# A graph, attention and experts layer on one core: conditional blocks placed inside two products, and rows of the experts' activations at 512-byte pitches

## The chip, the core and the metric

The kernel runs on one core of a Trainium2 chip. The profile names the core's engines PE (TensorE: matrix products; its weight loads are a row of their own, PEld), DVE (VectorE), ACT (ScalarE), POOL (GpSimd) and SP (SyncE, which here issues DMAs). An engine's own sequencer, which loads registers, compares and branches, is written with a q behind the name (PEq, DVEq). The metric is the device time of one execution in microseconds (us), lower being better; the kernel before took 1030.24 us, the median of three runs (1027.24 to 1032.03).

## The reference, cut to what matters

The input is a matrix x of 625 nodes by 1024, and 20000 edges `src -> dst`. Two sub-layers are added to x.

```python
xn = _layernorm(x, axis=-1)
x = x + _L0_gnn_ref(xn, src, dst, ...) + _L0_mix_ref(xn[None], Wq, Wk, Wv, Wo, bo)[0]
x = x + _L0_ffn_ref(_layernorm(x, axis=-1)[None], router_w, w1, w2, shared_gate_up, shared_down, shared_gate_w)[0]
```

`_L0_gnn_ref` is two graph layers: each is `h @ W_self + mean @ W_neigh + b`, where `mean` is the average of the rows of h over the incoming edges of a node, and the first is followed by a relu. `_L0_mix_ref` is a linear attention of 16 heads: q, k and v products, softmaxes, a small 64 x 64 context for each head, and an output product with Wo. `_L0_ffn_ref` is a mixture of 8 experts, of which each token takes two, `silu(x @ w1[e]) @ w2[e]`, beside a shared pair of products whose last one is `shared_down`. All weight matrices are 1024 x 1024 in float32.

## The kernel before, in words

**Products.** Every float32 operand is split into a rounded part and a remainder (`split`, L96 to L97: a copy on ACT makes `whi`, a subtraction on DVE makes `wlo`), and a product is three matmuls: high by high, high by low, low by high. Weights come in tiles of 128 x 1024 through one list, the stream `st` (L100 to L148): SP issues a tile's DMA, ACT and DVE split it, PE uses it. Three split tiles may exist at once, and the raw tiles are fetched three (in the experts six) ahead. `ts_half` (L197 to L210) multiplies the 625 nodes, in five tiles of 128 rows, by one half (512 columns) of a weight matrix. It has four steps u, one weight tile each, and in each step 30 matmuls of 512 columns, which add into five PSUM banks. There are eight banks in all. A caller may pass `step`, which is called behind each u.

**Order of the work around the change.** Queries and values are multiplied; a count of the edges becomes the matrix `ath`; `psc` (L725) and DVE's scaling (L728) make the contexts `cbd`. Then stands the first conditional block (L731), then `psa` (L742), which applies the contexts to the queries and is split into `aoh`, `aol`, then the output product with Wo (`pso`, both halves), whose banks are added to x and the biases in `xr` (POOL L760, DVE L761) and stored to `accd` in HBM. Then comes the neighbours' product (`neighbours`, L766; banks `psg`), which is split into `g0h`, `g0l`; then the second block (L776); then the hidden layer (`psag`, L802). The neighbours' product of the second layer follows, and then the product with its W_self (`psx`, L830). Its banks are added to `x2`, which holds what was stored in `accd` (L834, L835). The third block (L836) stands behind it, in front of `last_mean` (`psm`, L857). Later come the router, the shared gate and up products, the eight experts, a fourth block (L1255), and the last product with `shared_down` (`psz`).

**What the blocks are for.** Edge counts are packed in a few bits. `look` (L550) finds whether a count was too large for that, and puts a number into `rare`; every engine loads it into a register (L730) and branches. With the data of the run `rare` is 0, so the first three blocks are skipped: the first would count again (`recount`) and turn the inverse degrees around once more (`inverse`), the second and the third would add what the packed counts leave out (`low_part`). The fourth block is a loop over experts whose tokens don't fit into their slots; its number is loaded at L1254, and it runs once more `expert_narrow` with weights of its own. It is skipped as well. The first three blocks are written with `preferred_fallthrough_block=False`, the fourth without it. Two tiles of `shared_down` are split ahead of the fourth block (`st.ready`, L1253).

**Experts.** The six fuller experts run through `expert_wide` (L1135), three of them with n = 224 rows and three with 160; the other two have 128 rows and run through `expert_narrow` (L1210). In `expert_wide` the activations `he` are held for each of eight k as n columns of the high part followed by the low part: 2n float32 in a row, 1792 bytes for 224 and 1280 bytes for 160. For 160 the low part is cut so that the remaining 32 rows' high and low parts lie side by side. The second product (`psy`, L1184 and L1206 to L1208) loads slices of `he` as PE's weights and streams the weight tiles of w2. `expert_narrow` holds its `he` in pieces of 128 columns, 512 bytes each.

**What orders the instructions.** A framework (Tile) places the instructions on the engines' queues, gives out slots of shared buffers, and sets all semaphores. A conditional block is one unit for it. Slots are given out by tag: the large tiles (`xnh`, `xnl`, `hself`, `aoh`, `aol`, `g0h`, `g0l`, `hth`, `htl`, `x2`, `he` and others) share six, `tmp` has five.

Of the kernel before, what the change touches and what calls it, by code (L numbers as in the profile page):

```python
# [71 lines left out]
def gps_layer(ctx: ExitStack, tc: tile.TileContext, x, src, dst,  # L72
# [91 lines left out]
    def add_ts(w):  # L164
        for ap in row_aps(w):
            st.add(ap)
# [2 lines left out]
    add_ws(ws0)  # L169
    add_ts(wq)  # L170
    add_ts(wv)
    add_ts(wo)
    add_ts(wn0)
    add_ts(wn1)
    add_ts(ws1)
    for o in range(KT):
# [20 lines left out]
    def ts_half(xh, xl, accs, first=True, last=True, step=None):  # L197
        for u in range(4):
            wh, wl = st.next()
            for t in range(NT):  # L200
                c, acc = cols(t), accs[t][rows(t), :]
                for k in range(2):
                    kt = 2 * u + k
                    f = first and kt == 0
                    s = last and kt == KT - 1
                    nc.tensor.matmul(acc, xh[:, kt, c], wh[:, k, :], start=f, stop=False)  # L206
                    nc.tensor.matmul(acc, xh[:, kt, c], wl[:, k, :], start=False, stop=False)  # L207
                    nc.tensor.matmul(acc, xl[:, kt, c], wh[:, k, :], start=False, stop=s)  # L208
            if step:
                step(u)  # L210

    def ws_tile(xh, xl, accs, parts, last=True, w=None, step=None):
        wh, wl = w or st.next()
# [411 lines left out]
    def inverse(t0, n):  # L625
        ps = bank("psd").rearrange("p (a b) -> p a b", b=128)
        for t in range(n):
            p = rows(t0 + t)
            nc.tensor.transpose(ps[:, t, p], degs[p, 2, t0 + t:t0 + t + 1].to_broadcast([p.stop, 128]), ident[p, p])
        c = slice(t0 * T, min((t0 + n) * T, N))  # L630
        nc.scalar.copy(dinv[:, c], ps.rearrange("p a b -> p (a b)")[:, :c.stop - c.start])
# [89 lines left out]
    for o in range(KT):  # L721
# [4 lines left out]
        for h in range(2):  # L726
            r = slice(h * 64, (h + 1) * 64)
            nc.vector.tensor_scalar(cbd[r, o, r], ps[r, r], krs[r, o:o + 1], None, op0=ALU.mult)  # L728

    rare_v = nc.values_load(rare[0:1, 0:1], min_val=0, max_val=2)  # L730
    with tc.If(rare_v > 0, preferred_fallthrough_block=False):  # L731
        recount()
        inverse(0, NT - 1)
        inverse(NT - 1, 1)


    aoh, aol = slot_t("aoh"), slot_t("aol")
# [13 lines left out]
    for half in range(2):  # L751
        hs = slice(half * 512, (half + 1) * 512)
        accs = [bank("pso") for _ in range(NT)]
        ts_half(aoh, aol, accs)
        for t in range(NT):
            xr = tmp.tile([128, 512], F32, name="xr", tag="tmp")
            p = rows(t)
            for r, q in pieces(t):
                nc.gpsimd.dma_start(xr[q], x[r, hs])
            nc.gpsimd.tensor_add(xr[p], xr[p], bsum[p, hs])  # L760
            nc.vector.tensor_add(xr[p], accs[t][p, :], xr[p])  # L761
            for r, q in pieces(t):
                nc.gpsimd.dma_start(accd[r, hs], xr[q])


    def neighbours(xh, xl, gh, gl):  # L766
        for half in range(2):
            hs = slice(half * 512, (half + 1) * 512)
            accs = [bank("psg") for _ in range(NT)]
            ts_half(xh, xl, accs)  # L770
            for t in range(NT):
                split(accs[t][rows(t), :], gh[rows(t), t, hs], gl[rows(t), t, hs])

    g0h, g0l = slot_n("g0h", F32R), slot_n("g0l", F32R)
    neighbours(xnh, xnl, g0h, g0l)
    with tc.If(rare_v > 0, preferred_fallthrough_block=False):  # L776
        for s in range(NT):
            al = low_part(s)
            for o in range(KT):
                for c0, n in PARTS:  # L780
                    ps = bank("pslo")
                    c = slice(c0, min(c0 + n, N))
                    nc.tensor.matmul(ps[:, :n], g0h[rows(s), s, o * 128:(o + 1) * 128], al[rows(s), c0:c0 + n],
                                     start=True, stop=True)
                    lt = tmp.tile([128, NP], F32, name="lt", tag="tmp")
                    nc.vector.tensor_mul(lt[:, c], ps[:, :min(n, N - c0)], dinv[:, c])
                    nc.vector.tensor_add(hself[:, o, c], hself[:, o, c], lt[:, c])

    hth, htl = slot_t("hth"), slot_t("htl")
    pad(hth, htl)  # L790
# [33 lines left out]
    g1h, g1l = slot_n("g1h", F32R), slot_n("g1l", F32R)  # L824
    neighbours(hth, htl, g1h, g1l)
    x2 = slot_n("x2")
    for half in range(2):
        hs = slice(half * 512, (half + 1) * 512)
        accs = [bank("psx") for _ in range(NT)]
        ts_half(hth, htl, accs)  # L830
        for t in range(NT):
            p = rows(t)
            for r, q in pieces(t):
                nc.gpsimd.dma_start(x2[q, t, hs], accd[r, hs])  # L834
            nc.vector.tensor_add(x2[p, t, hs], accs[t][p, :], x2[p, t, hs])  # L835
    with tc.If(rare_v > 0, preferred_fallthrough_block=False):  # L836
        for s in range(NT):
            al = low_part(s)
            for t in range(NT):
                for half in range(2):  # L840
                    hs = slice(half * 512, (half + 1) * 512)
                    ps = bank("pslo")
                    p = rows(t)
                    nc.tensor.matmul(ps[p, :], al[rows(s), cols(t)], g1h[rows(s), s, hs], start=True, stop=True)
                    nc.vector.scalar_tensor_tensor(x2[p, t, hs], ps[p, :], degs[p, 2, t:t + 1], x2[p, t, hs],
                                                   op0=ALU.mult, op1=ALU.add)
    xst = const.tile([128, NT, 2, 6], F32, name="xst")
    def turn(tiles):
        for t in tiles:
# [285 lines left out]
    def expert_wide(row, n, xs, between):  # L1135

        rest = n - 128
        beside = rest <= 64
        he = big.tile([128, KT, 2 * n], F32R, name="he", tag="big")
        main, more = n + (rest if beside else 0), n + (0 if beside else 128)  # L1140
        for q in range(KT // 2):
            ps = [bank("pse") for _ in range(2)]
            for g in range(2):
                wh, wl = st.next()
                for a in range(2):
                    for k in range(4):
# [12 lines left out]
            for a in range(2):  # L1159
                nc.scalar.copy(s[:, a, :], ps[a][:, n:2 * n])  # L1160
                nc.vector.tensor_add(s[:, a, :], ps[a][:, :n], s[:, a, :])
            nc.scalar.activation(s, s, AF.Silu)
            h2 = he[:, 2 * q:2 * q + 2]
            if beside:
                nc.scalar.copy(h2[:, :, :n], s)
                for a0, b0, m in ((0, main, 128), (128, more, rest)):
                    nc.vector.tensor_sub(h2[:, :, b0:b0 + m], s[:, :, a0:a0 + m], h2[:, :, a0:a0 + m].bitcast(F32))
            else:
                split(s, h2[:, :, :n], h2[:, :, n:])
        r = between() if between else None  # L1170
        for half in range(2):
            accs = [bank("psy") for _ in range(2)]
            for u in range(4):
                wh, wl = st.next()
                rows_product(accs[0], lambda kt, p: he[:, kt, p * main:p * main + 128], u, wh, wl)
                if beside:

                    for k in range(2):
                        kt = 2 * u + k
                        f, e = kt == 0, kt == KT - 1  # L1180
                        both = (accs[1][:2 * rest], he[:, kt, 128:128 + 2 * rest], wh[:, k, :])
                        low = (accs[1][:rest], he[:, kt, 128:n], wl[:, k, :])
                        for m in (low, both) if e else (both, low):
                            nc.tensor.matmul(*m, start=f and m is both, stop=e and m is both)  # L1184
                else:
                    rows_product(accs[1][:rest], lambda kt, p: he[:, kt, 128 + p * n:n + p * n], u, wh, wl)
            expert_out(row, accs[:1], half, nc.vector.tensor_copy)
            y = tmp.tile([128, 512], F32, name="y", tag="tmp")
            if beside:
# [62 lines left out]
    st.load(st.used + st.ahead)  # L1252
    st.ready = [st.next(), st.next()]  # L1253
    n_over = nc.values_load(oi[0:1, OVB:OVB + 1], min_val=0, max_val=OVB)  # L1254
    with tc.If(n_over > 0):  # L1255
        with tc.For_i(0, n_over, 1) as j:
            ej = nc.values_load(oi[0:1, ds(j, 1)], min_val=0, max_val=NE - 1)
            row = REG + j * 128
# [58 lines left out]
```

## Time and profile before

| what | value |
|---|---|
| median of three runs | 1030.24 us (1027.24 to 1032.03) |
| the profiled execution | 1032.83 us, of which 1031.2 us are its span; 1.6 us lie around it |
| mean granted TensorE clock | 0.989 |
| PE, PEld, DVE, ACT, POOL busy | 1004.8, 866.2, 595.3, 397.7, 160.2 us |
| instructions | 14763 |
| `psc`, `psa`, `pso` | from 269.15, 279.08, 287.35 us of the span |
| first neighbours' product, hidden layer | from about 342, from 398.02 us |
| `psx` both halves, `last_mean` | from about 477, from 531.44 us |
| experts, last product | from about 680, from 970.12 us |

The span is the time from the first instruction to the last. A row of the groups gives a line of the kernel, the engine, the operation, the tiles written and read, its busy time, the mean duration of one, and the idle time ahead of it with what ended that. The view of waits says which engine waited for which other and for how long; "issue" there is idle time in which the profile shows nothing that the engine waited for. In the timeline the first column is the start and the second the length; matmuls overlap, so the time that one costs in a row of them is the distance between two starts. In the table by stretches each engine's busy time is followed by the granted TensorE clock (1.00 is full speed), the busy share of the DMA engines and the GB/s that they moved.

### The profile page before, as it was taken

To read this page: it belongs to the slowest core of one execution; us is meant where nothing else is said; L and a number is where in the kernel's file an instruction comes from. 1 tells how busy PE (TensorE), PEld (TensorE's weight loads), DVE (VectorE), ACT (ScalarE), POOL (GpSimd) and SP (SyncE) were. 2 spreads that over 40 slices of the span, in tenths; PEclk is the share of its full clock that TensorE was granted. 3 is DMA by queue.
4 is the path that set the end of the run, shared out by engine and by line. 5 is a ranking of instruction groups with operands and counts; after the bars stand their busy time and mean duration, and the time that the engine had idled before them with its cause. 6 is when DMAs were issued, how large, how long until landed. Compare 5 with 4: busy or idle time off the path is not lost. (4 is left out here: it accounts for less than half of the span.)

```text
span 1031.2 us, 14763 instructions
## 1 busy us (share of the span) xinstructions
PE 1004.8 (97%) x5543; PEld 866.2 (84%) x5543; DVE 595.3 (58%) x1216; ACT 397.7 (39%) x583; POOL 160.2 (16%) x216
## 2 busy tenths in 40 slices
PE   7999999999999999999999999999999999999798
PEld 5999998888888888888877999997988787887686
DVE  6999644472433335423337354457776788887571
ACT  5443242232221122222115242355656666776410
POOL 4100001120145100200001004203031033200210
PEclk8999999999999999999999999999999999999899
DMA  7122236663235311322220127467877898888951
GB/s 208 42 83 70 75 104 243 225 223 110 90 105 182 129 66 61 121 81 82 81 63 2 42 82 280 134 208 203 267 249 218 288 306 275 280 279 268 325 186 50
DMA packets 111463, 164.67 MB, mean 160 GB/s; under 512 B 5931, under 2 KB 63443, under 8 KB 111382
## 3 DMA queue, kind: packets, MB, share of 16 engines
q1 hardware_dynamic: 97734, 118.38, 36.0%
q0 software_dynamic: 13456, 45.08, 13.2%
q8 instruction: 46, 0.75, 0.3%
q14 instruction: 35, 0.29, 0.1%
q10 hardware_dynamic: 192, 0.16, 0.0%
HBM read 133.19 MB, written 30.42 MB: 159 GB/s over the span
## 5 line engine op out<-in xcount | busy, mean ns | idle before, releaser
L97 DVE TENSOR_TENSOR wlo<-wraw,whi 128x1024 fp32r<-128x1024 f32 x146 | 185.0, 1267 | 266.3 <-ACT whi L97 262.0
L97 ACT CAST whi<-wraw 128x1024 fp32r<-128x1024 f32 x149 | 156.5, 1050 | 304.0 <-PE psg L208 66.2
L1155 PE MATMUL pse<-xs,whi 128*128 128x448 f32 (+1 forms) x384 | 108.9, 357 | 0.0
L97 DVE TENSOR_TENSOR wlo<-wmore,whi 128x1024 fp32r<-128x1024 f32 x67 | 86.9, 1298 | 30.0 <-ACT whi L97 29.2
L97 ACT CAST whi<-wmore 128x1024 fp32r<-128x1024 f32 x67 | 70.4, 1051 | 53.4 <-PE psz L208 24.3
L1151 PE MATMUL pse<-xs,wlo 128*128 128x224 f32 (+1 forms) x384 | 89.6, 254 | 0.3 <-DVE wlo L97 0.3
L392 PE MATMUL psk<-xnh,whi 128*128 128x314 f32 (+3 forms) x256 | 82.9, 325 | 0.2 <-ACT xnh L97 0.2
L393 PE MATMUL psk<-xnl,whi 128*128 128x314 f32 (+3 forms) x256 | 79.6, 311 | 0.0
L394 PE MATMUL psk<-xnh,wlo 128*128 128x314 f32 (+3 forms) x256 | 79.6, 311 | 0.0
L1151 PEld LDWEIGHTS pse<-xs,wlo 128*128 128x128 f32 x384 | 71.9, 190 | 1.4 <-DVE wlo L97 0.5
L1207 PE MATMUL psy<-wlo,he 128*128 128x512 f32 (+1 forms) x176 | 70.0, 398 | 3.2 <-DVE wlo L97 2.9
L1155 PEld LDWEIGHTS pse<-xs,whi 128*128 128x128 f32 x384 | 69.0, 189 | 2.4
L1206 PE MATMUL psy<-whi,he 128*128 128x512 f32 (+1 forms) x176 | 69.4, 395 | 0.0
L1208 PE MATMUL psy<-whi,he 128*128 128x512 f32 (+1 forms) x176 | 69.1, 393 | 0.0
L97 POOL TENSOR_TENSOR xs<-raw,xs 128x512 fp32r<-128x512 f32 (+2 forms) x24 | 35.5, 1502 | 117.0 <-ACT xs L97 96.3
L392 PEld LDWEIGHTS psk<-xnh,whi 128*128 128x128 f32 x256 | 49.6, 194 | 0.5 <-ACT xnh L97 0.5
L474 DVE TENSOR_SCALAR hot<-iota,srow,unit 125x128 f16<-125x128 f16 x160 | 49.8, 311 | 0.0
L393 PEld LDWEIGHTS psk<-xnl,whi 128*128 128x128 f32 x256 | 49.6, 194 | 0.0
L394 PEld LDWEIGHTS psk<-xnh,wlo 128*128 128x128 f32 x256 | 49.4, 193 | 0.0
L1207 PEld LDWEIGHTS psy<-wlo,he 128*128 128x128 f32 (+1 forms) x176 | 31.8, 181 | 14.7 <-DVE wlo L97 6.5
L1206 PEld LDWEIGHTS psy<-whi,he 128*128 128x128 f32 (+1 forms) x176 | 31.9, 181 | 10.1
L473 DVE TENSOR_SCALAR hot<-iota,edt 125x128 f16<-125x128 f16 x160 | 40.1, 251 | 0.2 <-issue 0.2
(347 smaller groups left out, 2353.6 us busy)
## 6 DMA issues: line engine op xcount, KB each, us to landing
wraw<-in_L_ffn_w_dram SPq DMA_DIRECT2D x65, 512.0 KB, 5.1
wmore<-in_L_ffn_w_dram SPq DMA_DIRECT2D x63, 512.0 KB, 5.5
xsd<-zt POOLq DMA_DIRECT2D x9, 1024.0 KB, 5.2
wraw<-in_L_gnn_W_self_dram SPq DMA_DIRECT2D x16, 512.0 KB, 3.6
wraw<-in_L_gnn_W_neigh_dram SPq DMA_DIRECT2D x16, 512.0 KB, 3.8
wraw<-_ffn_shared_gate_up_dram SPq DMA_DIRECT2D x16, 512.0 KB, 3.9
wraw<-in_L_mix_Wk_dram SPq DMA_DIRECT2D x8, 512.0 KB, 5.5
wraw<-in_L_mix_Wq_dram SPq DMA_DIRECT2D x8, 512.0 KB, 3.7
```

The source lines that it names most:

```text
L97: return (order(nc.scalar.copy(hi, srcap)), order((eng or nc.vector).tensor_sub(lo, srcap, hi.bitcast(F32))))
L392: nc.tensor.matmul(ps[:, :n], wh[:, kt, :], xnh[:, kt, c], start=kt == 0, stop=False)
L393: nc.tensor.matmul(ps[:, :n], wh[:, kt, :], xnl[:, kt, c], start=False, stop=False)
L394: nc.tensor.matmul(ps[:, :n], wl[:, kt, :], xnh[:, kt, c], start=False, stop=kt == KT - 1)
L473: nc.vector.tensor_scalar(h[:ET, :WIN], iota[:ET, :WIN], edst[e], None, op0=ALU.is_equal)
L474: return nc.vector.tensor_scalar(h[:ET, WIN:], iota[:ET, :WIN], srow[e], unit[e].bitcast(F32), op0=ALU.is_equal, op1=ALU.mult)
L1151: nc.tensor.matmul(ps[a][:, :n], wl[:, k, c], xs[:, kt, 0, :], start=False, stop=False)
L1155: nc.tensor.matmul(ps[a][:, :2 * n], wh[:, k, c], xs[:, kt], start=kt == 0, stop=kt == KT - 1)
L1206: nc.tensor.matmul(acc, h(kt, 0), wh[:, k, :], start=kt == 0, stop=False)
L1207: nc.tensor.matmul(acc, h(kt, 0), wl[:, k, :], start=False, stop=False)
L1208: nc.tensor.matmul(acc, h(kt, 1), wh[:, k, :], start=False, stop=kt == KT - 1)
```

## The change

The change has four parts.

- **Order.** The first neighbours' product is moved ahead of `psa` and of the product with Wo; the weights' list has W_neigh ahead of Wo accordingly.
- **Two blocks become one inside a product.** The contents of the first and the second block stand in one block inside the product with Wo, second half, behind step u = 1. The third block moves into `psx`, second half, behind u = 1. In both, new matmuls inside the block (`hold`) add zeros to the five banks that the product has open. `x2` is loaded from `accd` ahead of each half of `psx`, not behind it.
- **The fourth block** gets `preferred_fallthrough_block=False`.
- **Pitches.** In `expert_wide` a row of `he` is 512 float32 (2048 bytes) for 224 rows and 384 (1536 bytes) for 160; the low part of the first 128 rows begins at column 256, the remaining rows' at 384 for 224 and, as before, at 160 for 160.

```diff
     add_ts(wv)
+    add_ts(wn0)
     add_ts(wo)
-    add_ts(wn0)
...
+    def hold(accs):
+
+        for t in range(NT):
+            nc.tensor.matmul(accs[t][rows(t), :128], zt[:, rows(t)], zt[:, :128], start=False, stop=False)
...
-    rare_v = nc.values_load(rare[0:1, 0:1], min_val=0, max_val=2)
-    with tc.If(rare_v > 0, preferred_fallthrough_block=False):
-        recount()
-        inverse(0, NT - 1)
-        inverse(NT - 1, 1)
...
     neighbours(xnh, xnl, g0h, g0l)
-    with tc.If(rare_v > 0, preferred_fallthrough_block=False):
+    rare_v = nc.values_load(rare[0:1, 0:1], min_val=0, max_val=2)
+
+    def low_parts():
         for s in range(NT):
             al = low_part(s)
...
+    def low_step(half, u, accs):
+        if (half, u) == (1, 1):
+            with tc.If(rare_v > 0, preferred_fallthrough_block=False):
+                recount()
+                inverse(0, NT - 1)
+                inverse(NT - 1, 1)
+                low_parts()
+                hold(accs)
...
+        ts_half(aoh, aol, accs, step=lambda u: low_step(half, u, accs))
...
+    def mean_low_step(half, u, accs):
+        if (half, u) != (1, 1):
+            return
+        with tc.If(rare_v > 0, preferred_fallthrough_block=False):
+            for s in range(NT):
+                al = low_part(s)
...
+            hold(accs)
...
         accs = [bank("psx") for _ in range(NT)]
-        ts_half(hth, htl, accs)
+        for t in range(NT):
+            for r, q in pieces(t):
+                nc.gpsimd.dma_start(x2[q, t, hs], accd[r, hs])
+        ts_half(hth, htl, accs, step=lambda u: mean_low_step(half, u, accs))
         for t in range(NT):
             p = rows(t)
-            for r, q in pieces(t):
-                nc.gpsimd.dma_start(x2[q, t, hs], accd[r, hs])
             nc.vector.tensor_add(x2[p, t, hs], accs[t][p, :], x2[p, t, hs])
-    with tc.If(rare_v > 0, preferred_fallthrough_block=False):
...
-        he = big.tile([128, KT, 2 * n], F32R, name="he", tag="big")
-        main, more = n + (rest if beside else 0), n + (0 if beside else 128)
+        he = big.tile([128, KT, 384 if beside else 512], F32R, name="he", tag="big")
+        main, more = 256, n if beside else 384
...
-                split(s, h2[:, :, :n], h2[:, :, n:])
+                split(s, h2[:, :, :n], h2[:, :, 256:256 + n])
...
-                    rows_product(accs[1][:rest], lambda kt, p: he[:, kt, 128 + p * n:n + p * n], u, wh, wl)
+                    rows_product(accs[1][:rest], lambda kt, p: he[:, kt, 128 + p * 256:n + p * 256], u, wh, wl)
...
-    with tc.If(n_over > 0):
+    with tc.If(n_over > 0, preferred_fallthrough_block=False):
```

More of the change, by code (lines that the diff above doesn't have):

```diff
@@ L728, in gps_layer, with neighbours @@
             nc.vector.tensor_scalar(cbd[r, o, r], ps[r, r], krs[r, o:o + 1], None, op0=ALU.mult)
-    rare_v = nc.values_load(rare[0:1, 0:1], min_val=0, max_val=2)
-    with tc.If(rare_v > 0, preferred_fallthrough_block=False):
-        recount()
-        inverse(0, NT - 1)
-        inverse(NT - 1, 1)
+    def neighbours(xh, xl, gh, gl):
+        for half in range(2):
+            hs = slice(half * 512, (half + 1) * 512)
+            accs = [bank("psg") for _ in range(NT)]
+            ts_half(xh, xl, accs)
+            for t in range(NT):
+                split(accs[t][rows(t), :], gh[rows(t), t, hs], gl[rows(t), t, hs])
+    g0h, g0l = slot_n("g0h", F32R), slot_n("g0l", F32R)
+    neighbours(xnh, xnl, g0h, g0l)
+    rare_v = nc.values_load(rare[0:1, 0:1], min_val=0, max_val=2)
+    def low_parts():
+        for s in range(NT):
+            al = low_part(s)
+            for o in range(KT):
+                for c0, n in PARTS:
+                    ps = bank("pslo")
+                    c = slice(c0, min(c0 + n, N))
+                    nc.tensor.matmul(ps[:, :n], g0h[rows(s), s, o * 128:(o + 1) * 128], al[rows(s), c0:c0 + n],
+                                     start=True, stop=True)
+                    lt = tmp.tile([128, NP], F32, name="lt", tag="tmp")
+                    nc.vector.tensor_mul(lt[:, c], ps[:, :min(n, N - c0)], dinv[:, c])
+                    nc.vector.tensor_add(hself[:, o, c], hself[:, o, c], lt[:, c])
+    def low_step(half, u, accs):
[6 more added lines that the diff above has]
+                hold(accs)
     aoh, aol = slot_t("aoh"), slot_t("aol")
@@ L753, in gps_layer @@
         accs = [bank("pso") for _ in range(NT)]
-        ts_half(aoh, aol, accs)
+        ts_half(aoh, aol, accs, step=lambda u: low_step(half, u, accs))
         for t in range(NT):
@@ L763, in gps_layer @@
                 nc.gpsimd.dma_start(accd[r, hs], xr[q])
[L766 to L787, printed above, removed]
     hth, htl = slot_t("hth"), slot_t("htl")
@@ L826, in gps_layer @@
     x2 = slot_n("x2")
+    def mean_low_step(half, u, accs):
+        if (half, u) != (1, 1):
+            return
+        with tc.If(rare_v > 0, preferred_fallthrough_block=False):
+            for s in range(NT):
+                al = low_part(s)
+                for t in range(NT):
+                    for h in range(2):
+                        hs = slice(h * 512, (h + 1) * 512)
+                        ps = bank("pslo")
+                        p = rows(t)
+                        nc.tensor.matmul(ps[p, :], al[rows(s), cols(t)], g1h[rows(s), s, hs], start=True, stop=True)
+                        nc.vector.scalar_tensor_tensor(x2[p, t, hs], ps[p, :], degs[p, 2, t:t + 1], x2[p, t, hs],
+                                                       op0=ALU.mult, op1=ALU.add)
+            hold(accs)
     for half in range(2):
@@ L829, in gps_layer @@
         accs = [bank("psx") for _ in range(NT)]
-        ts_half(hth, htl, accs)
+        for t in range(NT):
+            for r, q in pieces(t):
+                nc.gpsimd.dma_start(x2[q, t, hs], accd[r, hs])
+        ts_half(hth, htl, accs, step=lambda u: mean_low_step(half, u, accs))
         for t in range(NT):
             p = rows(t)
-            for r, q in pieces(t):
-                nc.gpsimd.dma_start(x2[q, t, hs], accd[r, hs])
             nc.vector.tensor_add(x2[p, t, hs], accs[t][p, :], x2[p, t, hs])
[L836 to L846, printed above, removed]
     xst = const.tile([128, NT, 2, 6], F32, name="xst")
```

## The prediction

> **What bounds the kernel now.** I read the page first. PE is busy for 1004.8 of 1031.2 us; no other engine passes 60%. The chain that ended last is all `psz` matmuls. So the end is set by PE's row of matmuls, and an edit counts only if it closes a gap of PE, keeps its clock, or shortens the distance between matmuls. PE's waits list all gaps:
>
> ```profile
> PE 1004.8 (97%) x5543; PEld 866.2 (84%) x5543; DVE 595.3 (58%) x1216; ACT 397.7 (39%) x583; POOL 160.2 (16%) x216
> ```
>
> ```profile
> PE psz L206 <- issue: 5.2, 1, 5.2
> ...
> PE psag L802 <- DVEq L776: 1.5, 1, 1.5
> ...
> PE psm L857 <- DVEq L836: 0.9, 1, 0.9
> PE psa L742 <- DVEq L731: 0.8, 1, 0.8
> ```
>
> These four stand at the four conditional blocks, three short ones behind a DVE sequencer and one of 5.2 us with no releaser. The timeline of PE and the table by stretches show what the last one costs:
>
> ```profile
> 964.57 0.39 PE L1208 MATMUL psy<-whi,he 128*128 128x512 f32 x1
> 970.12 0.77 PE L206 MATMUL psz<-whi,sth 128*128 128x512 f32 x1 [5.16 <-issue]
> 970.68 0.63 PE L207 MATMUL psz<-wlo,sth 128*128 128x512 f32 x1
> ...
> 974.79 0.39 PE L208 MATMUL psz<-whi,stl 128*128 128x512 f32 x1
> ```
>
> ```profile
> 968.00:970.00 2.00, 0.00 (x0) 0.00 (x0) 0.00 (x0) 0.00 (x0) 0.00 (x0) 0.50 0.68 209
> 970.00:972.00 2.00, 1.89 (x5) 1.53 (x6) 0.00 (x0) 0.00 (x0) 0.54 (x1) 0.50 0.98 321
> ```
>
> The granted clock is 0.50 from 968 on, and the eleven steps from 970.12 to 974.79 take 4.67 us. In `psx` 33 steps, from 522.25 to 529.73, take 7.48, 0.227 each; eleven of those are 2.5. So the gap costs 5.55 - 0.23 = 5.3 us and the low clock behind it 2.2.
>
> **Part 1, the fourth block.** The lines of L1255 and L836 side by side (sequencer, instruction, count, durations in ns, first and last start):
>
> ```profile
> L1255 PEldq EVENT_SEMAPHORE  x2: 51/51/51, 965.0 to 965.1; - x2
> L1255 PEldq COMPARE_BRANCH  x1: 330/330/330, 964.1 to 964.1; - x1
> ```
>
> ```profile
> L836 PEldq COMPARE_BRANCH  x2: 73/132/190, 526.4 to 530.8; - x2
> ...
> L836 PEldq EVENT_SEMAPHORE  x1: 51/51/51, 530.6 to 530.6; - x1
> ```
>
> At L1255 PE's sequencer is through at 965.15, 0.2 us behind its last matmul (964.96), and then nothing happens for five microseconds. The queue q8, which moves instructions (46 packets, 0.75 MB, so 16 KB each), carries one packet at 967 to 968 and another at 973; elsewhere among the experts 16 us or more lie between two. I read the gap as PE waiting for code beyond the skipped block. The three blocks that have the new layout already (two branches instead of one) show no such gap: PE goes on 0.8 to 1.5 us behind its last matmul, each time when DVE's sequencer has left. I therefore take the gap to shrink to what the other engines allow. The waits say that `psz` waited for ACT's sequencer at L1255, which leaves at 966.6, behind a split of 965.47 to 966.52; its DVE partner left at 966.4. With 0.15 us to start, `psz` begins at 966.75 instead of 970.12: **-3.4 us**. If ACT's split falls behind the block, only PE's own 0.7 us stay, and -4.5 is the other end; if the code still has to be fetched, 0.
>
> The clock: the new idle time is 1.8 us. Idle 1.46 us at 396.56 left the clock at 1.00. Matmuls ceased from 551.6 to 556.1, with transposes in between and 1.89 us of pure idle, and the clock then stood at 0.69, 0.50 and 0.96 in three stretches of 2 us, which cost (0.31 + 0.50 + 0.04) x 2 = 1.7 us. 1.8 us lies between these; with no transposes beside it I take the first, so the loss goes: **-2.2 us**, with -0.5 as the other end. [...]
>
> Behind it: POOL's gathers of `ys` begin at 971.46, behind the landing of the store issued at 966.84, and land until about 990. DVE needs them for the first half's banks, which finish near 994 instead of 1000. Four microseconds are left there, so the gain is not given back. SP's three late loads (967.9 to 969.1, landing in 5.7) are for tiles needed from 994 on.
>
> **Part 2, the blocks inside the products.** Removed are 0.82 + 1.46 + 0.86 = 3.1 us of idle PE. The real dependences behind them don't bind: the first `psag` needs only the first rows of `g0h` and six banks, of which three are free and three come out before the product ends; `psm` likewise; `psa` needs `cbd`, long done when a product of 54 us lies in between.
>
> Added are two stops. PE's event waits for its running matmuls, then the second branch runs: from the last matmul's end to the branch's end it was 0.45 us at L731 (278.26 to 278.71), 0.53 at L776, 0.41 at L836. ACT and DVE reach the block as soon as they have split the tiles ahead, six or more us before PE (ACT left L731 at 270.5, PE at 278.4), and step u = 2 needs nothing else. So 2 x 0.5 = 1.0: **-2.1 us** net. The ends are 0.4 each and, by the dearest row, 5.3 + 2.2 = 7.5 each, which counts as a rival.
>
> [...] The three rows above are blocks of which none stalled.
>
> Who queues behind the merged block: POOL. Its loads of `xr` for the second half (L759) now wait until PE has left the block, 13.6 us into that half (in the old one they waited 47.2 us for L731). Six issues of 0.55 us, 3.8 to land, then five adds of 1.38: the first bank's `xr` is ready 0.55 + 3.8 + 1.4 = 5.8 us after the block, the last one's 4.4 + 6.9 = 11.3. DVE wants them 8.2 and 13.6 us after it. So 2 us are spare and the cost is 0; with landings of 5.4 us and POOL's issues in between, +1.5. The DMAs for `x2` were issued at 422 already, long before `psx`: moving them costs nothing. The exchange of weights in the list moves equal tiles; `psa`, paced by PE (16 x 0.54 = 8.7 us), hides ACT's split of the last `g0h` bank (0.58) in front of its own. If that cover fails, 0.6 us.
>
> **Part 3, the pitches.** PE's weight loads from `he` take 188 ns at either layout, so there is nothing in them. But the steps differ: from 700.00 to 708.33, n = 224, 36 steps take 8.33, 0.2314 us each; with 128-column pieces, 957.29 to 964.57, 32 steps take 7.28, 0.2275, with the DMA engines fully busy. For n = 160 it is 0.230. Three experts x 96 matmuls x 3.9 ns + three x 80 x 2.5 ns = 1.7 us if the pitch is the reason. Against that, `pse` in an expert of 128 with aligned pieces also takes 0.231 (942 to 953). I take **-1.0 us**, between 0 and, with all steps at 0.2267, -2.2. DVE's and ACT's writes to `he` keep their counts of elements: 0.
>
> **Sum.** -3.4 - 2.2 - 2.1 - 1.0 = -8.7 us. From the profiled execution, 1032.83 (span 1031.2 and 1.6 around it), that is 1024.1; this execution lay 2.6 above the median of 1030.24, from which it is 1021.5. I give **1021.5**.
>
> **Rivals.**
>
> 1. *The fourth block's gap stays* (chance 0.10): the layout does not do what it says; for it speaks that nothing in the trace ties the gap to code but the timing of a queue. Then only parts 2 and 3 count: 1030.2 - 3.1 = 1027.1.
> 2. *One long stop inside a product* (0.08): the merged block, whose code is longest, stalls PE as L1255 did. -8.7 + 7.5 - 0.5 = -1.7: 1028.5. Against it: L731 holds most of that code and cost 0.8.
> 3. *Skipping costs a fetch wherever code is not near* (0.06), the slower end: one mechanism at all three blocks. The fourth keeps its gap, and both stops in the products take 7.5 instead of 0.5: -3.1 + 14.0 = +10.9, 1041. It decides for slower once the two stops together pass 4.1 us (3.1 of removed idle and 1.0 of pitch). Against it: the three rows with two branches each.
>
> The forecast has 0.76. **Range** 1016 to 1028.5. The ends of the sum are -4.5 - 2.2 - 2.3 - 2.2 = -11.2 (1019.0) and, with the clock dropping, POOL late and no gain from pitches, -3.4 - 0.5 - 0.6 = -4.5 (1025.7); the first two rivals are taken in above, and 3 us below for the runs' own spread (1027.24 to 1032.03). A change of 0.5% (5.15 us), about what a measurement of this kernel tells from none, lies at 1025.1 and 1035.4. Faster: 0.93 of the forecast and a bit of rival 1, 0.73; slower: rival 3, 0.06; the rest, 0.21, within.
>
> **What would show it.** Right: no wait of `psz` beyond 2 us, clock 1.00 around it; no wait at `psa`, `psag`, `psm`; one gap of about 0.5 us in `pso` and in `psx`, each behind 60 matmuls of the second half; steps of `psy` at 0.228. Wrong: `psz` still idle 4 us or more with "issue"; a gap over 2 us in `pso` or `psx`, or a clock below 1.00 behind one; `psag` waiting for DVE's adds at L761; steps of `psy` unchanged.

## The result, and the profile after

The changed kernel takes 1027.55 us (median of 7 runs, 1027.07 to 1029.95), the kernel before beside it 1031.21 (7 runs, 1027.24 to 1032.92): ratio 0.9975, 95% interval 0.9961 to 0.9988. The change gains 2.6 us by the ratio, where 8.7 were forecast. The profiled execution took 1029.63 us with a span of 1027.9, 3.3 less than the span before.

The page's line of busy time and PE's waits, which answer to the first lines shown of before:

```profile
PE 1002.9 (98%) x5543; PEld 865.1 (84%) x5543; DVE 596.3 (58%) x1216; ACT 397.3 (39%) x583; POOL 158.2 (15%) x216
```

```profile
PE pso L206 <- issue: 3.6, 1, 3.6
...
PE psz L206 <- DVEq L1272: 1.5, 1, 1.5
...
PE psx L206 <- PEq L841: 0.6, 1, 0.6
```

The waits at `psa`, `psag` and `psm` are gone, and `psz` waits 1.5 us in place of 5.2. But the wait that has no releaser ("issue") is still there. It now stands inside `pso`, at the merged block (L763 in the changed kernel; the `psx` block is L841, the fourth L1272). PE's timeline around it, and the table by stretches (the granted clock is the third number from the end):

```profile
381.63 0.39 PE L208 MATMUL pso<-whi,aol 128*113 128x512 f32 x1
385.57 0.50 PE L206 MATMUL pso<-whi,aoh 128*128 128x512 f32 x1 [3.56 <-issue]
...
387.06 0.63 PE L208 MATMUL pso<-whi,aol 128*128 128x512 f32 x1
387.48 0.63 PE L206 MATMUL pso<-whi,aoh 128*128 128x512 f32 x1
```

```profile
386.00:388.00 2.00, 2.00 (x8) 1.56 (x7) 0.00 (x0) 0.00 (x0) 2.00 (x2) 0.65 0.82 272
388.00:390.00 2.00, 2.00 (x6) 1.56 (x5) 0.00 (x0) 0.00 (x0) 1.96 (x3) 0.50 0.91 296
```

From one matmul's start to the next's it is 3.94 us instead of 0.23, and eight steps behind it take 0.43 instead of 0.23: 3.7 + 1.7 = 5.4 us, where the prediction had 0.5. The rows of the merged block for PE's sequencer say where it stood: its second branch alone took 3309 ns (columns as before: count, shortest, median and longest duration in ns, first and last start).

```profile
L763 PEldq COMPARE_BRANCH  x2: 98/1704/3309, 378.4 to 382.2; - x2
```

All other engines had left by 378.1. Between 381.7 and 385.6 the DMA queues show one 16-KB packet of instructions (queue, kind: packets, MB, share):

```profile
q8 instruction: 1, 0.02, 1.5%
```

At the fourth block there is no packet in the gap, and the clock stays whole:

```profile
966.98 0.39 PE L1225 MATMUL psy<-whi,he 128*128 128x512 f32 x1
968.81 0.47 PE L206 MATMUL psz<-whi,sth 128*128 128x512 f32 x1 [1.45 <-DVEq L1272]
```

```profile
968.00:970.00 2.00, 1.19 (x5) 1.04 (x6) 1.15 (x2) 0.93 (x1) 0.54 (x1) 1.00 0.62 238
```

So the time went like this, from the starts of the stages. From the start of `psc` to the end of `last_mean`'s first group (the stretch that holds part 2) it was 278.77 us before and is 281.26 now: **+2.5**, forecast -2.1. The gap at the fourth block shrank by 3.7, and 2.1 of low clock went (the 240 steps of `psz` take 54.3 us in place of 56.4): **-5.8**, forecast -5.6. The second products of the six wide experts took 123.85 us and take 123.47: **-0.4**, forecast -1.0. The sum is -3.7, of which the span shows -3.3; the rest lies in differences of a few tenths elsewhere.

### The profile page after: what moved, and what is told of

The parts are those of the page before. It is cut to its first block, busy times and chain, and to the rows that moved or that the text cites. A ratio compares the mean times of both kernels' runs of the same rounds, so it can differ in the third digit from the quotient of the medians.

```text
span 1027.9 us, 14759 instructions
## 1 busy us (share of the span) xinstructions
PE 1002.9 (98%) x5543; PEld 865.1 (84%) x5543; DVE 596.3 (58%) x1216; ACT 397.3 (39%) x583; POOL 158.2 (15%) x216
```

## The experiments

First theory (A): PE stops because it jumps over the merged block's code, which is longer than any block before. Rival (B): it is what stands in the block. The expectations give 443 instructions for it and 105 to 264 for the blocks before; some weight loads are counted twice there. From the branch to the code behind the block it is 429 instructions, and 107 to 250 at the three short stops before.

### Four kernels on the first theory

**e1_split**: the merged block cut in two.

```diff
-        if (half, u) == (1, 1):
+        if (half, u) == (1, 0):
             with tc.If(rare_v > 0, preferred_fallthrough_block=False):
                 recount()
                 inverse(0, NT - 1)
                 inverse(NT - 1, 1)
+                hold(accs)
+        if (half, u) == (1, 1):
+            with tc.If(rare_v > 0, preferred_fallthrough_block=False):
                 low_parts()
                 hold(accs)
```

> The changed kernel with its merged block cut in two, both inside pso: recount and the two inverses after step (half 1, u 0), low_parts after step (1, 1), each with its own hold; nothing else differs. Theory A (TensorE stops because its sequencer has to jump over the merged block's 443 instructions, where the jumps over 105 to 264 cost nothing visible): two stops of 0.6 to 1.0 us and a clock of 1.00 behind them, so 5.4 us lost becomes 1.2 to 2.0 and the run is 3.4 to 4.2 us under the changed kernel, a profiled span near 1024. Theory B (it is what stands in the block, the recount inside a running product): the block with recount alone still stops TensorE by over 3 us, and the run is 0 to 1 us over the changed kernel, for the second stop comes on top.

Measured: 1024.86 us against 1029.27 before, ratio 0.9956 (0.9940 to 0.9973). Its waits:

```profile
PE psz L206 <- DVEq L1275: 1.5, 1, 1.5
...
PE pso L206 <- PEq L769: 0.6, 1, 0.6
...
PE pso L206 <- PEq L763: 0.6, 1, 0.6
PE psx L206 <- PEq L844: 0.6, 1, 0.6
```

Two short stops stand where the long one was, and the recount alone does not stop PE: this speaks against B. By the ratios the gain over the changed kernel is 2.0 us (0.9975) to 3.4 (0.9989, e8_after), where 3.4 to 4.2 were expected. The cut also moves the first half 60 instructions ahead, so it doesn't tell the length from the place.

**e3_longpsx**: a longer block elsewhere.

```diff
-            for s in range(NT):
+            for s in [s for _ in range(4) for s in range(NT)]:
                 al = low_part(s)
```

> The changed kernel with the loop in the psx block's code repeated four times (431 instructions of TensorE in place of 116; the block is not entered with these inputs, so nothing more is computed). Theory A (length of the code jumped over): the stop inside psx grows from 0.73 to 3 to 4.5 us and a low clock follows for some 3 us, 4 to 5.5 us over the changed kernel. Theory B (content: no recount stands here): the stop stays at 0.6 to 1.0 us and the time within 0.5 us of the changed kernel.

Measured: 1032.72 us, ratio 1.0038 (1.0022 to 1.0055). Two long stops now:

```profile
PE psx L206 <- issue: 4.0, 1, 4.0
PE pso L206 <- issue: 3.7, 1, 3.7
```

The second branch of L841 takes 3702 ns in place of 310, and one instruction packet lies in this stop too. Next to the changed kernel's 0.9975 that is some 6 us more, over the 4 to 5.5 that A gave. The block starts where it did; only its end has moved. A holds so far.

**e2_fourth**: the flag alone.

```diff
-    with tc.If(n_over > 0):
+    with tc.If(n_over > 0, preferred_fallthrough_block=False):
```

> The kernel before with the fourth block's flag alone (its code laid out aside). By the two traces this part gives 3.7 us of gap between the last expert product and the shared product and 2.3 us of clock behind it: 6.0 us under the kernel before, a gap of 1.8 us and no step of the clock under 1.00 behind it. The rival, that the gap shrank because of the longer program or the other blocks' new places ahead of it: a gap of over 3 us and a gain of under 3 us.

Measured: 1029.33 us, ratio 0.9995 (0.9983 to 1.0007): nothing. The gap is there, with a packet in it, and the clock is at 0.50 from 968 to 974:

```profile
965.01 0.39 PE L1208 MATMUL psy<-whi,he 128*128 128x512 f32 x1
970.03 0.77 PE L206 MATMUL psz<-whi,sth 128*128 128x512 f32 x1 [4.63 <-issue]
```

This went against my reading of part 1, and against A as well, for the block is of the same length here and in the changed kernel.

**e4_pitch**: the pitches alone, put into the kernel before.

> The kernel before with the pitches of he alone (256 floats between the high and the low part for every wide expert). The six wide experts' products took 123.85 us before and 123.47 in the changed kernel: 0 to 0.5 us under the kernel before, the profiled time not to be told from it. The prediction's own step said 1.0 us.

Measured: 1028.80 us, ratio 0.9999 (0.9988 to 1.0009). The six products take 123.48 us, 0.37 less than before. Part of that is spread: in all sixteen profiles the three products of 224 rows take 67.52 to 67.55 us with the old pitch and 67.25 to 67.32 with the new, those of 160 rows 56.2 to 56.4 with either. So the pitches are worth 0.2 to 0.3 us. The fourth block has 3.49 us of idle PE here, with a packet in it.

### A second theory: where the block falls between fetches

What differs between e2_fourth and the changed kernel at the fourth block is its place: 17 instructions later (in PE's program 11095 instructions stand ahead of it before, those of skipped blocks included, and 11112 after). Queue q8 carries one packet of 16 KB for some 256 instructions that PE executes in a steady product (in the changed kernel four packets for 1025 between 243.60 and 350.63 us; single ones come after 250 to 264, where the expectations say 254 to 257). So I shifted all blocks by putting small matmuls behind the warm-up, where PE waits for the first tile anyway (in the changed kernel `pst` waits 2.1 us for ACT's `xts` up to 9.44 us, and 0.6 up to 9.38 with the 14 matmuls ahead of it in e6); each is a load and a matmul, two instructions.

```diff
         nc.tensor.matmul(psw, cold[:, :128], cold, start=i == 0, stop=i == WARM - 1)
+    for i in range(14):
+        nc.tensor.matmul(psw[:, :64], cold[:, :128], cold[:, :64], start=True, stop=True)
```

**e5_shift_before**: this in the kernel before.

> The kernel before with nothing changed but 14 small matmuls (64 columns, into the warm-up bank that nobody reads) behind the warm-up: 28 more instructions of TensorE ahead of every block, in time that TensorE spends waiting for the first tile. The traces show TensorE's instruction-fetch packets of 16 KB, one for each 254 to 257 instructions. Where TensorE stopped at a block for over 3 us, a fetch packet lies inside the stop, and the block's branch had come 17 to 24 instructions after the last such boundary (the fourth block of before, its flagged copy, and the merged block); where it stopped 1.4 us, 46 to 85 instructions after it. Theory C (a stop is long when the branch meets code that is still being fetched, so it is set by where the block falls between two fetches): the unflagged fourth block now comes some 50 instructions after a boundary, its gap falls from 5.5 to about 2 us and no low clock follows, 3 to 6 us under the kernel before. Theory D (the layout: code first costs the gap, whatever its place): the gap stays over 3 us and the time within 1 us of before.

Measured: 1028.12 us against 1032.22, ratio 0.9959 (0.9945 to 0.9972). The unflagged block, code first:

```profile
963.57 0.39 PE L1210 MATMUL psy<-whi,he 128*128 128x512 f32 x1
965.40 0.47 PE L206 MATMUL psz<-whi,sth 128*128 128x512 f32 x1 [1.45 <-DVEq L1257]
```

The clock is 1.00 from 964 to 970, and no packet lies in the gap. Fourteen matmuls whose result nobody reads gain what I had put down to the flag.

**e6_shift_after**: the same in the changed kernel.

> The changed kernel with the same 14 small matmuls behind the warm-up, so that the merged block's branch comes 49 instructions after a fetch boundary in place of 21 and its end still falls in the next 256. Theory C (place between fetches): the stop at the merged block falls from 3.6 to 0.6 to 1.0 us, no low clock follows, the other two stops stay at 0.6 and 1.5: 4 to 5 us under the changed kernel. Theory A (length of the code jumped over): 443 instructions still stop TensorE for over 3 us, and the time is within 1 us of the changed kernel.

Measured: 1026.28 us, ratio 0.9949 (0.9929 to 0.9968). The block has its 429 instructions, and the long stop is gone:

```profile
PE psag L814 <- DVE xr L797: 1.2, 1, 1.2
PE pso L206 <- PEq L765: 0.7, 1, 0.7
```

A falls as it stood, and B with it: length and contents are those of the changed kernel. A new wait of 1.2 us shows at `psag`, to which I return.

**e7_split_noflag**: e1_split without the flag at the fourth block.

> The kernel with the merged block cut in two, with the fourth block's flag taken back (its code stands first again, as before), at an unchanged place: 64 instructions after a fetch boundary. Theory C: the gap at the fourth block stays near 1.8 to 2.3 us and the time within 1 us of the kernel cut in two. Theory D (the flag itself removes the gap): the gap is back at 5 us with a low clock behind it, 5 to 6 us over the kernel cut in two.

Measured: 1028.08 us against 1032.22, ratio 0.9964 (0.9952 to 0.9977); the gap at the fourth block has 1.43 us of idle PE, as with the flag (1.45):

```profile
PE psz L206 <- DVEq L1275: 1.4, 1, 1.4
```

At a good place the layout makes no difference, as at the bad one (e2_fourth). D falls.

**e8_after**: the changed kernel again.

> The changed kernel once more, unaltered, as the reference for the others on this chip: 2 to 4 us under the kernel before, with stops of about 3.6, 0.6 and 1.5 us at its three blocks if these follow from the program alone and not from the execution.

Measured: 1030.76 against 1032.22, ratio 0.9989 (0.9972 to 1.0006): 1.1 to 1.5 us, less than the 2 to 4 expected. The stops are 3.5, 0.6 and 1.9 us. But behind the long one the clock is not lowered this time:

```profile
385.50 0.50 PE L206 MATMUL pso<-whi,aoh 128*128 128x512 f32 x1 [3.54 <-issue]
```

```profile
386.00:388.00 2.00, 2.00 (x11) 1.59 (x10) 0.00 (x0) 0.00 (x0) 2.00 (x2) 1.00 0.79 272
```

**e9_shift100**: a control, `WARM = 14` in place of 20 and 56 small matmuls, 100 instructions in all.

> The changed kernel with six of the twenty warm-up matmuls replaced by 56 small ones: 100 instructions more ahead of the blocks in place of 28. The merged block's branch then comes some 121 instructions after a fetch boundary, and its 429 to 443 instructions end in the second fetch after the one that it stands in. Theory C (where the block and its end fall between the fetches): the long stop at the merged block is back, 3 us or more, with a fetch packet inside it, while the psx block (some 51 after a boundary) and the fourth (some 146) stop 0.6 and 1.5 us: within 1.5 us of the changed kernel, 3 to 5 us over the kernel with 28 instructions more. The rival, that any small matmuls behind the warm-up help, by the clock or by an earlier start: stop of 0.6 us and the time of the kernel with 28 more.

Measured: 1032.29 us against 1031.43, ratio 1.0002 (0.9992 to 1.0013). `pso` waits 3.7 us again, `psx` 0.4 and `psz` 1.5:

```profile
PE pso L206 <- issue: 3.7, 1, 3.7
```

The time is 6.9 us over the kernel with 28 more (e11, on the same chip), more than the 3 to 5 expected: the small matmuls help by the place that they give the block, not by themselves.

**e10_step_earlier**: `(half, u) == (1, 0)` in `low_step`, `WARM = 14` and 54 small matmuls.

> The changed kernel with the merged block one step earlier in pso (half 1, u 0 in place of 1, 1), and six warm-up matmuls replaced by 54 small ones so that its branch comes some 57 instructions after a fetch boundary (the psx block some 47, the fourth some 142). Theory C: stops of 0.6 to 1.0, 0.6 and 1.5 us and no low clock behind them. The loads of xr for half 1, which POOL issues only when TensorE has passed the block, start some 7 us earlier, and the 1.2 us that psag waits for xr in the kernel with 28 instructions more goes: 1.0 to 1.5 us under that kernel, 5 to 7 under the kernel before. The rival, that the wait at psag comes from the additions of VectorE themselves: psag still waits 1 us and the time is that of the kernel with 28 more.

Measured: 1025.01 us against 1031.43, ratio **0.9939** (0.9927 to 0.9952); span 1022.0. No long stop, no wait at `psag`:

```profile
PE psz L206 <- DVEq L1274: 1.4, 1, 1.4
...
PE pso L206 <- PEq L765: 0.6, 1, 0.6
...
PE psx L206 <- PEq L843: 0.4, 1, 0.4
```

**e11_shift_again**: e6_shift_after once more.

> The changed kernel with 28 instructions more ahead of its blocks once more, in more rounds, as the reference for the two others: 4 to 5 us under the kernel before, stops of 0.65, 0.55 and 1.5 us, a wait of 1.2 us for xr at psag. If theory C is wrong and the first run of it was chance, the stop at the merged block is back at 3 us or more.

Measured: 1025.44 us, ratio 0.9946 (0.9932 to 0.9960). The stops are as expected, but `psag` doesn't wait here. So the wait at `psag` comes in one execution and not in the next, and e10_step_earlier gains 0.4 us on this kernel and not 1.0 to 1.5; the two intervals overlap.

**e12_shift12**: six small matmuls, 12 instructions.

> The changed kernel with 6 small matmuls behind the warm-up: 12 more instructions ahead of the merged block in place of none (stop 3.56 us) or 28 (stop 0.65). Theory C taken as a sum: the fetch is asked for when TensorE's sequencer crosses a boundary, and the stop is what is left of it when the branch comes. Twelve instructions are six matmuls of 0.227 us, 1.4 us more of head start, so the stop at the merged block is 1.8 to 2.5 us, no low clock need follow, and the time is 1.5 to 3.5 us under the changed kernel. The rival, that a branch close behind a boundary loses the fetch under way and begins it anew: a stop of 3 us or more, as with no shift.

Measured: 1029.66 us against 1031.59, ratio 0.9988 (0.9971 to 1.0005). The stop did not shrink:

```profile
PE pso L206 <- issue: 4.1, 1, 4.1
```

My sum was wrong and its rival right in the number. At the merged block the stop is whole or absent: 3.6 and 3.5 us with no shift, 4.1 with 12 instructions, 0.65 with 28, 0.65 with 36 (e10_step_earlier: 96 more, and the block 60 earlier), 3.65 with 100.

**e13_before_plus8** and **e14_before_minus8**: the kernel before with four small matmuls (8 instructions more), and with `WARM = 16` (8 fewer).

> The kernel before with 4 small matmuls behind the warm-up, 8 instructions more ahead of its blocks (28 more took the fourth block's gap from 5.5 to 1.8 us). Theory C1 (a stop is long when the jump's end lies in the second fetch after the branch's own; the fourth block is 255 to 258 instructions long, so that holds at a few places only): the gap falls to about 1.8 us and the time is 2 to 5 us under the kernel before. Theory C2 (a stop is long when the branch comes within some 30 instructions behind a boundary, as the counts of records seem to say): eight instructions are not enough, the gap stays over 3 us, the time within 1 us of the kernel before.

> The kernel before with 16 warm-up matmuls in place of 20: 8 instructions fewer ahead of its blocks. Theory C1: the jump ends some 8 instructions short of where it did, in the last few of the fetch that is there, so TensorE comes out of the block after 1.4 to 2 us and stops again some 3 to 6 matmuls into the shared product, while the next fetch, which is asked for only when the jump lands, is on its way: 1 to 4 us there, in sum 0 to 3 us under the kernel before. Theory C2: the branch comes 8 instructions closer behind the boundary and the gap at the block itself stays over 3 us.

Measured: e13 1031.36 us against 1030.54, ratio 1.0001 (0.9981 to 1.0021), 3.90 us of idle PE at the block:

```profile
PE psz L206 <- PEq L1257: 3.9, 1, 3.9
```

e14 1030.34, ratio 0.9999 (0.9985 to 1.0013). In e14 the stop comes in two pieces:

```profile
963.94 0.47 PE L206 MATMUL psz<-whi,sth 128*128 128x512 f32 x1 [1.66 <-ACTq L1255]
964.25 0.40 PE L207 MATMUL psz<-wlo,sth 128*128 128x512 f32 x1
967.51 0.79 PE L208 MATMUL psz<-whi,stl 128*128 128x512 f32 x1 [2.87 <-issue]
```

PE leaves the block, does two matmuls and stops in the middle of a row of matmuls, where no branch stands: C1 had said three to six. With eight instructions fewer the jump still ends in code that is there, and a packet comes within the second stop (965.30, 2.2 us before PE goes on at 967.51). I take it that the next packet begins four instructions on (two matmuls with their loads), and that the end of the jump was just at a packet's edge in the kernel before. C2, which wanted the whole gap at the block, falls by this. But C1 had 1.8 us for e13 and it was 3.9, so C1 falls too as a rule for all places. What fits all, as my reading of these runs and not as a row that shows it, is this: a stop is long when the jump ends in, or close ahead of, a packet that has not come yet, either because the end lies two packets on, or because the next packet is too late.

The packets in the traces agree with it. In each of the eleven stops of over 2.5 us one packet begins while PE stands still, and PE goes on 2.2 to 3.4 us later (in the kernel before the packet begins at 967.62 and PE goes on at 970.12, in the changed kernel at 383.18 and 385.57). At the merged block with a shift of 0 or 12 instructions (the changed kernel, e8, e3, e12) no packet had come for 31 us ahead of the second branch, and the next began 1.0 us behind it (in the changed kernel packets at 350.63 and 383.18, the branch at 382.2). With 28 and 36 (e6, e11, e10) one had come 5.2 to 5.8 us ahead. In e9, with 100, one had come 13.1 us ahead and the stop was long all the same: there the jump ends one packet further on, by my count of instructions.

### What the runs say together

| stops of over 2.5 us at a block, in the profiled execution | kernels and ratios to before |
|---|---|
| none | e10 0.9939, e11 0.9946, e6 0.9949, e1 0.9956, e5 0.9959, e7 0.9964 |
| one | the changed kernel 0.9975 and 0.9989, e12 0.9988, e2 0.9995, e4 0.9999, e14 0.9999, e13 1.0001, e9 1.0002 |
| two | e3 1.0038 |

By these ratios each kernel without a long stop is faster than each kernel with one, whichever of the changes it has (the intervals of neighbours in the list overlap). The kernel before has one, the changed kernel has one: the change moved it from the fourth block to the merged one.

## Why the prediction was wrong

**Part 2, the step that failed**: "So 2 x 0.5 = 1.0". The `psx` block cost 0.7, near the 0.5 forecast; the merged one cost 5.4. That was rival 2, which had 0.08; it gave 1028.5. The measured 1027.55 lies inside the stated range only because the range had taken that rival in; the sum's own ends were 1019.0 and 1025.7. I had set it aside because "L731 holds most of that code and cost 0.8". The runs show why the row was no evidence: with length and contents unchanged, the stop at the merged block was 3.56 us, and 0.65 with 28 instructions more ahead of it, so a row of one place says nothing on another. As I read it, what counts is where the jump's end falls between the packets. A jump over 429 instructions leaves the packet that it starts in, if one holds the 250 to 264 counted, and at three of the five places tried it stalled (with 0, 12 and 100 instructions more, not with 28 and 36).

By that count e9's jump ends two packets on. At shifts of 0 and 12 the jump ends in the very next packet, and the stop was as long; that packet had not come yet, it began 1.0 us behind the branch. The price was 3.5 to 4.1 us of idle PE at the merged block. I had taken for evidence three rows where no jump was over 250 instructions long, and those rows could not speak against a stop behind a longer one.

**The rest of part 2 was right.** The waits of 0.82, 1.46 and 0.86 us went. In e11 and e10, with no long stop, nothing else became late, and the stretch from `psc` to `last_mean` takes 276.78 and 276.61 us in place of 278.77: -2.0 and -2.2, where the step said -2.1. In e1, with three short stops there, it is 277.56, and in e6, with the wait at `psag`, 278.22. The loads of `xr` behind the block were priced at 0, "with landings of 5.4 us and POOL's issues in between, +1.5"; e6 shows 1.2 us in one execution, e11 and e10 none. In the changed kernel the long stop hid it.

**Part 1: the right size for the wrong reason.** Forecast -5.6, found -5.8 in the trace. That the gap is PE waiting for code fits the packet in it at 967.62, but I held the layout responsible. The flag alone gave nothing (e2, 4.63 us of idle PE), taking it away cost nothing (e7, 1.43), and a shift of 28 instructions without it left 1.45 of the 5.16 us (e5). That the gap went in the changed kernel because the code ahead of the block had grown by 17 instructions is argued from these runs; a shift of 17 alone was not run. One reading was off as well: the packets among the experts come down to 14.6 us apart (874.69 and 889.26), not 16. Rival 1 was, by its mechanism, true of the flag: "the layout does not do what it says".

**The clock** was right at the fourth block (no low clock behind 1.45 us of idle PE). The 2.2 us of low clock that rival 2 put behind a long stop were 1.7 at the merged block in the first trace and nothing in e8; in e3, e9 and e12 a low clock follows again. What went with it stands at the end.

**Part 3** was mis-sized: -1.0 forecast, 0.2 to 0.3 found over all profiles. The pitch accounts for about 0.001 us of a step (22.31 to 22.19 us for the third expert of 224, 96 such matmuls), not for 0.0039, and for nothing at 160 rows; what makes the rest of the difference was not tried.

**What stays open.** How many instructions behind the start of a packet a branch must stand so that the next one has come. At the fourth block 8 instructions more left 3.9 us and 17 left 1.5; at the merged block 12 left 4.1 and 28 left 0.65. The packets' times are known to some ten instructions only, and at the fourth block the weights of the last product are being fetched at the same time (the DMA engines were busy to 0.98 from 964 to 966 in e5), which may delay a packet; that was not tried by itself. Nor is it shown that a stop is the same in every execution: most kernels left one trace, and one of e13's ten executions took 1023.19 us, 4.4 under its next, without one.

## What to carry to other kernels

A skipped conditional block stopped the engine for 3.5 to 5.2 us here, and whether it did hung on 28 instructions far ahead of it (e5 and e6; in e6 they run at 8.2 us of the span and the block stands at 381; 12 did not shrink the stop there); look in the gap for an instruction packet and at the length of the sequencer's last branch before explaining it by the block. "Issue" alone is not enough: in e11 `psup` waits 1.0 us so at 631 us, with no packet between 614 and 637, and why is open. Before a gain or a loss at a branch is put down to an edit, move the same block by a few instructions with nothing else changed: here this was worth -4.1 us of itself in the kernel before (e5), more than the whole change. A longer jump can cost more (in e3 the `psx` block, longer by 315 instructions and with the same start, cost 4.0 us of wait in place of 0.6, with a packet in the stop), but a short one is no safeguard (the fourth block has 255 to 258, and PE stood idle there for 5.16 us). So run the version at more than one place.

## What was not expected of the hardware

- **PE stopped where no branch stands**: in e14 two matmuls after the block, for 2.87 us, with a packet coming in while it stands.
- **The same stop was followed by the low clock in one execution and not in the other.** 3.56 and 3.54 us of idle PE stood ahead of a clock of 0.50 for 3.41 us in the changed kernel and of 1.00 in e8. In the records of the granted clock of all sixteen profiles, a stretch at 0.50 inside the kernel lasts 3.4 or 6.8 us, and within a profile all changes lie whole multiples of 3.413 us apart (in the changed kernel 170.67, 3.41, 194.56, 3.41 and 167.25 us: 50, 1, 57, 1 and 49 of them; before, 170.67, 3.41, 361.81, 3.41, 409.60 and 6.83: 50, 1, 106, 1, 120 and 2). Cut into pieces of that length along these changes, the first of the two stops leaves 2.38 us of idle PE in one piece, the second 1.94 and 1.60 in two. Over all profiles, each of the ten pieces at full clock with 2.09 us (e14) or more of idle PE (2.82 at the fourth block before) was followed by one at 0.50; at the blocks, no piece at full clock with 1.94 or less was. Ten of the eleven long stops hold such a piece, and no stop of 1.45 us can.
- Two stretches at 0.50 come and go near 188 and 555 us of the span, where PE does transposes and very small matmuls, whatever the kernel (before, 3.41 us each from 189.54 and 554.76): the first is there in e6 and not in e11, which is the same kernel. A stretch of 3.4 us costs up to 1.7, as measured behind the merged block, a good part of the spread of one kernel's times (1027.24 to 1032.92 before).

The prediction had compared lengths of idle time, as if these alone decided: 1.46 us that kept the clock, 1.89 that lost it. By these records it was the idle time within one piece that went with the low clock at the blocks, and a piece did not have to be idle throughout: in e14 2.09 of 3.41 us stood ahead of the low clock.
